# Padding the rows of three large scratch tensors in memory

## The chip, the cores and the metric

The kernel runs on one core of one Trainium2 chip. The metric is the device time of one execution in microseconds (us). All data are 32-bit floats.

## The reference, cut to what matters

The input is 16 images of 16 channels, 256 x 256. Two layers follow each other, each added to its own input:

```python
x = x + _L0_conv_ref(_gn(x), L0_conv_weight)
x = x + _L1_conv_ref(_gn(x), ty, tx, weights_pole1, weights_pole2, weights_residue)
```

`_gn` normalizes groups of two channels. The first layer is a 3 x 3 circular convolution with 16 by 16 channels, written in the reference with Fourier transforms. The second is a Laplace neural operator: a 2D Fourier transform `alpha` of every channel, at every frequency a 16 x 16 complex matrix that mixes the channels, an inverse transform, and a second sum of exponentials built from the poles:

```python
alpha = jnp.fft.fft2(x, axes=(-2, -1))
S = jnp.einsum('ikpq,oikp,xikq->oxik', weights_residue, A, Bm)
output_residue1 = jnp.einsum('biox,oxik->bkox', alpha, S)
x1 = jnp.fft.ifft2(output_residue1, s=(Ny, Nx), axes=(-2, -1)).real
...
return x1 + x2 / Nx / Ny
```

## The kernel before, in words

The work goes through four stages, and what one stage leaves for the next is too large for the on-chip memory. It is kept in three scratch tensors in HBM:

- `vD`, four tensors of 128 x 16 channels x (4 images, 2, 256): the result of the first layer, folded into sums and differences of mirrored rows. The first index is the row pair, and one channel's part for it is 8 KB.
- `aD`, 128 x 32 x 4096: the spectrum. The first index is the frequency along y; of its 32 rows two (real and imaginary part) belong to each channel, and a row of 16 KB holds all 256 frequencies along x of all 16 images.
- `yD`, 128 x 32 x (4, 4, 256): the mixed rows, with the same first two indices, a row again 16 KB.

Stage 1, the convolution, is a loop over `g`, 24 steps for each of the 16 images (`conv`, L283). Small matmuls (L297) fill `ps_conv`; ScalarE evicts them to `pair` and `far` (L316); VectorE and GpSimd fold the mirrored rows (`mirror`, L264 and L267); SyncE stores `vD<-pair` (L326) and loads the images two ahead, `xt<-in_x` (L123). Stage 2, the spectrum, goes over 64 units of one channel and four images: `load_v` (L737) reads `s<-vD` three units ahead, `fold`, `lines` (L768, L776) and `columns` (L811) make the transform, and after four units, so once for each channel, L967 stores the 4 MB tile `spec` to `aD`.

Stage 3 mixes. It is a loop over 32 groups `g` of four frequencies, and in each over four steps `n`. A step makes the next group's weights (`sums`, L1024, `spread`), mixes with the present ones (`mix`, L1112), evicts four PSUM tiles to `yt` (L1225), stores `yt` (`store`, L1126, four DMAs of 128 KB in pieces of 1 KB) and loads a part of the next group's spectrum (`load`, L1094 and L1099, pieces of 2 and 1 KB):

```python
for m in range(4):
    o, src = mix(4 * n + m, sg, yt)
    (nc.vector.tensor_copy if m >= (2 if late else 3) else nc.scalar.copy)(o, src)
...
store(g, n, yt)
if g < 31:
    load(g + 1, n, (2, 3) if n == 1 else range(4))
```

`yt` has two buffers, so the eviction of step `n + 2` needs the stores of step `n` landed. `unmix_first` reads the first frequency's rows back from `yD` at the end of the stage, corrects them and writes them again (L1139, L1149).

Stage 4 is the inverse, over 16 channels `k` and four images at a time. Channel 0's rows of `yD` are read in pieces of 256 bytes (`load_images`, L1275), those of later channels a quarter at a time, 1 MB in pieces of 8 KB (`load_quarter`, L1294). `combine` (L1317, L1321) makes `u` on GpSimd, L1353, L1377 and L1378 transform, VectorE adds v (`vl<-vD`, L1302), and L1391 stores the output.

The order of the instructions is written out by hand in each stage. Nearly all transfers are issued by SyncE, in program order, and each waits until the one eight before it has landed.

Of the kernel before, what the change touches and what calls it, by code (L numbers as in the profile page):

```python
# [9 lines left out]
FP = mybir.dt.float32  # L10
# [6 lines left out]
B = 16  # L17
C = 16
N = 256
P = 128  # L20
# [4 lines left out]
def conv_then_laplace_kernel(ctx: ExitStack, tc: tile.TileContext, a: dict, out: bass.AP):  # L25
# [16 lines left out]
    x = a["x"]  # L42

    cp = ctx.enter_context(tc.tile_pool(name="const", bufs=1))
    dp = ctx.enter_context(tc.tile_pool(name="scratch", bufs=1, space=DRAM))
# [17 lines left out]
    proj = cp.tile([P, 2, B, 16, 2], FP, name="proj", tag="proj")  # L63
    jmat = cp.tile([P, 3, P], FP, name="jmat", tag="jmat")

    vD = [dp.tile([P, C, 4, 2, N], FP, name=f"vD{b}", tag=f"vD{b}") for b in range(B // 4)]
    aD = dp.tile([P, 2 * C, N * B], FP, name="aD", tag="aD")
    yD = dp.tile([P, 2 * C, 4, 4, 16 * B], FP, name="yD", tag="yD")
    cD = dp.tile([P, 4, 8, N], FP, name="cD", tag="cD")
    hD = dp.tile([7, 2, 16, C * C * 4], FP, name="hD", tag="hD")  # L70
    eD = [dp.tile([n, P, C, 2, P], FP, name=f"eD{n}", tag=f"eD{n}") for n in (2, 1)]
# [606 lines left out]
    for g in range(24 * B + 3):  # L678
# [3 lines left out]
        b, n = divmod(g, 24)  # L682
        if b + 2 < B and n % 12 in (4, 5, 10, 11):
            h, k = n // 12, (4, 5, 10, 11).index(n % 12)
# [47 lines left out]
    m, n = cols[:, 16:17], cols[:, 17:18]  # L732

    def load_v(i, b0, eng=nc.sync):
        s = sp.tile([P, 4, 2, N], FP, name="s", tag="s")
        for j in range(0, 4, 2):
            eng.dma_start(out=s[:, j : j + 2], in_=vD[b0 // 4][:, i, j : j + 2])  # L737
        return s.rearrange("p b h x -> p h b x")

    def fold(i, b0, s):  # L740


        vf = f1.tile([P, 2, 2, 4, P], FP, name="vf", tag="vf")
        lo, hi = s[:, :, :, 0:P], s[:, :, :, N - 1 : P - 1 : -1]
        for j in range(4):
            nc.vector.scalar_tensor_tensor(
                vf[:, 0, 0, j], lo[:, 0, j], vmr[:, 1, b0 + j, i : i + 1], hi[:, 0, j], ALU.add, ALU.add
            )
        nc.vector.tensor_tensor(vf[:, 0, 1], lo[:, 1], hi[:, 1], ALU.add)


        vq = fp.tile([P, 2, 2, 4, 2, 64], FP, name="vq", tag="vq")

        def again(xo, eng):
            lo, hi = vf[:, xo, :, :, 0:64], vf[:, xo, :, :, P - 1 : 63 : -1]
            eng.tensor_tensor(vq[:, xo, :, :, 0], lo, hi, ALU.add)  # L756
            eng.tensor_tensor(vq[:, xo, :, :, 1], lo, hi, ALU.subtract)  # L757

        again(0, nc.vector)
        nc.vector.tensor_tensor(vf[:, 1], lo, hi, ALU.subtract)  # L760
        again(1, nc.gpsimd)
        return vq.rearrange("p e o b h x -> p e o b (h x)")

    def lines(i, b0, vf, t, j):

        for xo in range(2):
            ps = pa.tile([P, 512], FP, name="ps_y", tag="ps_y")
            nc.tensor.matmul(  # L768
                ps[:, 0:N],
                lhsT=vf[:, xo, 0, j],  # L770
                rhs=tabE[:, 0 : i + 2 : i + 1],
                start=True,
                stop=False,
                skip_group_check=True,
            )
            nc.tensor.matmul(  # L776
                ps[:, P : P + N],
                lhsT=vf[:, xo, 1, j],
                rhs=tabO[:, i : C + 1 : C - i],
                start=False,  # L780
                stop=True,
                skip_group_check=True,
            )
            nc.scalar.activation(  # L784
                t[:, xo, j].rearrange("p l n -> p (l n)"),
                ps[:, 0:384],
                AF.Copy,
                scale=vmr[:, 0, b0 + j, i : i + 1],
            )
# [44 lines left out]
    def first_slots(b0, spec, pairs, qs):  # L834

        flat = spec.rearrange("p r f b -> p (r f) b")
        for (j, even, odd), q in zip(pairs, qs):
            bs = slice(b0 + j, b0 + j + 2)
            nc.vector.tensor_copy(flat[:, 0:385:384, bs], even[:, :, 0])
            nc.gpsimd.tensor_tensor(  # L840
                flat[:, 256:127:-128, bs],
                q[:, :, 0],
                sgn.unsqueeze(2).to_broadcast([P, 2, 2]),
                ALU.mult,
            )

    def project(i, psd):
        for part in range(2):
            cf = coef[part][:, i].rearrange("p k q s -> p (k q s)")
            cf = cf.unsqueeze(1).to_broadcast([P, B, 32])  # L850
            ac = proj[:, part].rearrange("p b m s -> p b (m s)")
            if i == 0:
                nc.vector.tensor_tensor(ac, psd, cf, ALU.mult)
            else:
                pr = prp.tile([P, B, 32], FP, name="pr", tag="pr")
                nc.vector.tensor_tensor(pr, psd, cf, ALU.mult)
                nc.gpsimd.tensor_tensor(ac, ac, pr, ALU.add)
# [20 lines left out]
    def first_constants():  # L878
        omega(omg, omg, rd[:, 1:2])
        nc.vector.tensor_scalar(pims, p2k[:, :, 1], sset, None, ALU.mult)  # L880
        nc.vector.tensor_tensor(prU[:, 0], p2k[:, :, 0], p2k[:, :, 0], ALU.mult)

        nc.vector.tensor_scalar(prU[:, 1], p2k[:, :, 0], m0, -1.0, ALU.mult, ALU.mult)
        nc.vector.tensor_scalar(prU[:, 2], p2k[:, :, 0], m1, -1.0, ALU.mult, ALU.mult)
# [50 lines left out]
    for u in range(len(units) + 1):  # L935
        at = units[u] if u < len(units) else None
        if at is not None:
            now = vq
            t = lp.tile([P, 2, 4, 3, P], FP, name="t", tag="t")
            if u + 1 < len(units):  # L940
                vq = fold(*units[u + 1], loaded.pop(u + 1))
                if u + 3 < len(units):
                    loaded[u + 3] = load_v(*units[u + 3])
                if u < 2:
                    next(rest)
            for j in range(2):
                lines(*at, now, t, j)
        if last is not None:
            i, b0 = last[:2]
            if b0 == 0:  # L950
                spec = (a0, a1)[i % 2].tile([P, 2, N, B], FP, name="spec", tag="spec")
                psd = pd.tile([P, B, 32], FP, name="psd", tag="psd")
            done = columns(*last, spec, psd)
        if at is not None:
            for j in range(2, 4):
                lines(*at, now, t, j)
                if u < 2:
                    next(rest, None)
        if u == len(units) - 4:
            first_constants()  # L960
        if len(units) - 4 < u < len(units):
            next(first_weights)
        if last is not None:
            first_slots(b0, spec, *done)
            if b0 == B - 4:
                project(i, psd)
                (nc.sync if i + 1 < C else nc.scalar).dma_start(  # L967
                    out=aD[:, 2 * i : 2 * i + 2].rearrange("p r n -> p (r n)"),
                    in_=spec.rearrange("p r f b -> p (r f b)"),
                )  # L970
        last = (*at, t) if at is not None else None
    p1.close()
# [443 lines left out]
    for n, (k, b0) in enumerate(units):  # L1416
# [13 lines left out]
        r = rp.tile([P, 4, 2, N], FP, name="r", tag="r")  # L1430
# [169 lines left out]
```

## Time and profile before

| | us |
|---|---|
| median of 3 runs | 2666.38 (2654.53 to 2671.68) |
| the profiled execution | 2667.82 |
| its span, first to last instruction | 2665.7 |
| TensorE busy | 2487.3 (93%) |
| VectorE busy | 1986.5 (75%) |
| ScalarE busy | 1447.7 (54%) |
| GpSimd busy | 1324.7 (50%) |
| SyncE's DMA queue, share of 16 engines | 71.7% |

The profile is of one execution. "PE" is TensorE, "PEld" its weight loads, "DVE" VectorE, "ACT" ScalarE, "POOL" GpSimd and "SPq" the queue of SyncE. "L1112" is a line of the kernel. A line with an arrow, as in `PE ps_mix L1112 <- DMA yD<-yt`, names an instruction that waited and what released it; "issue" stands for waiting that no event of the profile explains. The DMA share is the mean busy share of the core's 16 DMA engines.

### The profile page before, as it was taken

The page shows a single profiled execution, that of the slowest core. Times are in us where ns is not written, and L with a number is a line of the kernel's source. Part 1 is how long each engine was busy: PE and PEld are TensorE (multiplying, and loading weights), DVE is VectorE, ACT ScalarE, POOL GpSimd, SP SyncE. Part 2 cuts the span into 40 slices and gives each one's busy share as a digit, 9 for nine tenths or more (in the row PEclk, how much of TensorE's full clock was granted, in tenths as well). Part 3 has the DMA queues.
Part 4 walks back from the last instruction along what each step waited for, and adds up shares of the span by engine and source line. Part 5 has one row for each costly group of instructions (what it writes and reads, how often), then busy time and mean ns, then how long its engine had stood idle before and what let it go on. Part 6 is the DMA issues. An engine that isn't in the chain of part 4 may idle for free.

```text
span 2665.7 us, 83901 instructions
## 1 busy us (share of the span) xinstructions
PE 2487.3 (93%) x35314; PEld 1883.0 (71%) x35314; DVE 1986.5 (75%) x3805; ACT 1447.7 (54%) x2727; POOL 1324.7 (50%) x1179
## 2 busy tenths in 40 slices
PE   5988999898999999998999999999699999999998
PEld 2544444466777777775777878888588888888887
DVE  7767778847888888888787878888367666666666
ACT  2555566575666666665666666666244444444443
POOL 1333358432333333334476655776546565665653
PEclk9999999998999999999999999999899999999999
DMA  8888778955565556555777777777878888888884
GB/s 271 266 271 269 263 243 284 286 181 188 214 239 224 200 222 237 217 195 217 222 225 217 232 232 216 231 225 234 245 276 288 285 287 292 280 294 275 301 282 171
DMA packets 311351, 653.11 MB, mean 245 GB/s; under 512 B 44566, under 2 KB 159382, under 8 KB 301120
## 3 DMA queue, kind: packets, MB, share of 16 engines
q1 hardware_dynamic: 309936, 640.55, 71.7%
q8 instruction: 278, 4.55, 0.7%
q0 software_dynamic: 896, 3.02, 0.4%
q10 hardware_dynamic: 144, 4.19, 0.4%
q14 instruction: 97, 0.79, 0.1%
HBM read 368.15 MB, written 280.36 MB: 243 GB/s over the span
## 4 chain that ended last, share of the span: by engine, by line
PE 63%; DMA 4%; SPq 3%; DVE 3%; ACT 1%; issue 1%; POOL 1%; DVEq 0%; ACTq 0%; POOLq 0%
PE ps_mix L1112 11%; PE ps_y L768 9%; PE ps_p L1353 9%; PE ps_y L776 8%; PE ps_f L1377 8%; PE ps_f L1378 8%; PE ps_x L811 4%; DMA yD<-yt 3%; PE ps_s L1024 3%; PE ps_h L1337 2%; SPq L1126 2%; PE psd L796 1%; SPq L1094 1%; DVE sg L1044 1%; ACT yt L1225 0%
## 5 line engine op out<-in xcount | busy, mean ns | idle before, releaser
L1112 PE MATMUL ps_mix<-abd,sg 128*64 128x128 f32 x8192 | 481.1, 276 | 36.6 <-DMA yD<-yt 19.2
L1112 PEld LDWEIGHTS ps_mix<-abd,sg 128*64 128x64 f32 x8192 | 451.1, 138 | 90.2 <-ACT yt L1225 56.8
L297 PE MATMUL ps_conv<-xt,wc 32*32 32x512 f32 x12288 | 453.0, 618 | 57.6 <-issue 49.6
L1317 POOL TENSOR_TENSOR u<-yk 128x512 f32<-128x512 f32 (+1 forms) x268 | 350.1, 1338 | 291.1 <-PE ps_p L1353 223.9
L297 PEld LDWEIGHTS ps_conv<-xt,wc 32*32 32x32 f32 x12288 | 255.1, 105 | 243.3 <-issue 160.7
L784 ACT ACTIVATE t<-ps_y,vmr 128x384 f32<-128x384 f32 x512 | 297.0, 580 | 163.7 <-PE ps_y L776 163.6
L1044 DVE STREAM_SHUFFLE sg<-ps_s 128x512 f32<-128x512 f32 (+1 forms) x264 | 328.9, 1316 | 0.0
L768 PE MATMUL ps_y<-tabE,vq 128*128 128x256 f32 x1024 | 313.5, 388 | 13.6 <-DVE vq L757 12.1
L267 POOL TENSOR_TENSOR pair<-pair,far 128x1024 f32<-128x1024 f32 x64 | 151.6, 2369 | 345.8 <-DVE pair L264 285.6
L776 PE MATMUL ps_y<-tabO,vq 128*128 128x256 f32 x1024 | 306.0, 380 | 0.0
L1377 PE MATMUL ps_f<-pt,inv 128*128 128x256 f32 x1008 | 301.3, 381 | 0.0
L1378 PE MATMUL ps_f<-hs,ey 128*128 128x256 f32 x1008 | 300.5, 380 | 0.0
L1353 PEld LDWEIGHTS ps_p<-inv,u 128*128 128x128 f32 x2048 | 266.3, 193 | 47.2 <-issue 25.5
L1381 DVE TENSOR_TENSOR r<-ps_f,q 128x256 f32<-128x256 f32 x256 | 107.0, 418 | 254.0 <-ACT q L1380 254.0
L1353 PE MATMUL ps_p<-inv,u 128*128 128x128 f32 x2048 | 279.6, 280 | 10.0 <-POOL u L1321 9.9
L1041 ACT ACTIVATE sg<-ps_s,mcol 128x512 f32<-128x512 f32 (+1 forms) x264 | 179.8, 691 | 193.5 <-DVE sg L1044 123.9
L768 PEld LDWEIGHTS ps_y<-tabE,vq 128*128 128x128 f32 x1024 | 189.7, 191 | 90.1 <-ACT q L824 50.3
L1380 ACT COPY q<-ps_f 128x256 f32<-128x256 f32 x256 | 95.4, 372 | 288.8 <-PE ps_f L1378 284.7
L756 POOL TENSOR_TENSOR vq<-vf 128x512 f32<-128x512 f32 x64 | 81.4, 1271 | 295.0 <-DVE vf L760 272.4
L1355 ACT COPY pt<-ps_p 128x512 f32<-128x512 f32 x256 | 150.0, 586 | 134.2 <-PE ps_p L1353 129.9
L776 PEld LDWEIGHTS ps_y<-tabO,vq 128*128 128x128 f32 x1024 | 195.6, 191 | 27.0
L1225 ACT COPY yt<-ps_mix 128x512 f32<-128x512 f32 x352 | 184.8, 591 | 51.2 <-DMA yD<-yt 35.2
(239 smaller groups left out, 4056.3 us busy)
## 6 DMA issues: line engine op xcount, KB each, us to landing
vD<-pair SPq DMA_DIRECT2D x128, 512.0 KB
yD<-yt SPq DMA_DIRECT2D x512, 128.0 KB
vl<-vD SPq DMA_DIRECT2D x128, 512.0 KB
out_y<-ol SPq DMA_DIRECT2D x128, 512.0 KB
s<-vD SPq DMA_DIRECT2D x126, 512.0 KB
aD<-spec SPq DMA_DIRECT2D x15, 4096.0 KB
yk<-yD SPq DMA_DIRECT2D x60, 1024.0 KB
xt<-in_x SPq DMA_DIRECT2D x96, 516.0 KB
```

Source lines behind the costliest of these rows:

```text
L297: nc.tensor.matmul(acc[r][32 * c : 32 * c + 32], lhsT=ready[b][0][rows, phase, tap], rhs=halves[b][u // 2][rows, q : q + 5 : 4, 2 - tap : ...
L768: nc.tensor.matmul(ps[:, 0:N], lhsT=vf[:, xo, 0, j], rhs=tabE[:, 0 : i + 2 : i + 1], start=True, stop=False, skip_group_check=True,)
L776: nc.tensor.matmul(ps[:, P : P + N], lhsT=vf[:, xo, 1, j], rhs=tabO[:, i : C + 1 : C - i], start=False, stop=True, skip_group_check=True,)
L784: nc.scalar.activation(t[:, xo, j].rearrange("p l n -> p (l n)"), ps[:, 0:384], AF.Copy, scale=vmr[:, 0, b0 + j, i : i + 1],)
L1041: nc.scalar.activation(to[..., k : k + 2], src[odd], AF.Copy, scale=nsgn)
L1044: nc.vector.stream_shuffle(to[..., C + k : C + k + 2], src[1 - odd], swap)
L1112: nc.tensor.matmul(ps[64 * t : 64 * t + 64, j], lhsT=sg[:, f : f + 2].rearrange("p f m -> p (f m)"), rhs=abd[jq][:, :, 2 * t + cc, 2 * jj ...
L1225: (nc.vector.tensor_copy if m >= (2 if late else 3) else nc.scalar.copy)(o, src)
L1317: nc.gpsimd.tensor_tensor(u[:, :, j].rearrange("p b (c n) -> p c b n", c=8), in0, in1, o)
L1353: nc.tensor.matmul(ps[:, at], lhsT=u[:, n], rhs=tab, start=True, stop=True)
L1377: nc.tensor.matmul(ps[:, e], lhsT=tab, rhs=pt[:, e], start=True, stop=False)
L1378: nc.tensor.matmul(ps[:, e], lhsT=ey[:, e], rhs=hs, start=False, stop=True)
```

## The change

Behind each row of `aD` and `yD` now lie 256 unused numbers (1 KB), and behind each frequency's 32 rows another 1024 (4 KB). Behind each channel's 8 KB of `vD` lie 256 unused numbers. The distance from row to row grows from 16 to 17 KB in `aD` and `yD`, from frequency to frequency from 512 to 548 KB, in `vD` from channel to channel from 8 to 9 KB and from row pair to row pair from 128 to 144 KB. The store of the spectrum names its two rows one by one, since they no longer touch. All else is as it was.

```diff
-    vD = [dp.tile([P, C, 4, 2, N], FP, name=f"vD{b}", tag=f"vD{b}") for b in range(B // 4)]
-    aD = dp.tile([P, 2 * C, N * B], FP, name="aD", tag="aD")
-    yD = dp.tile([P, 2 * C, 4, 4, 16 * B], FP, name="yD", tag="yD")
+    def pitched(name, rows, row, *split):
+
+        t = dp.tile([P, rows * (row + 256) + 1024], FP, name=name, tag=name)
+        t = t[:, 0 : rows * (row + 256)].rearrange("p (r n) -> p r n", r=rows)[:, :, 0:row]
+        return t.rearrange("p r (i j n) -> p r i j n", i=split[0], j=split[1]) if split else t
+
+    vD = []
+    for b in range(B // 4):
+        t = dp.tile([P, C, 8 * N + 256], FP, name=f"vD{b}", tag=f"vD{b}")
+        vD.append(t[:, :, 0 : 8 * N].rearrange("p c (b h x) -> p c b h x", b=4, h=2))
+    aD = pitched("aD", 2 * C, N * B)
+    yD = pitched("yD", 2 * C, N * B, 4, 4)
...
                 (nc.sync if i + 1 < C else nc.scalar).dma_start(
-                    out=aD[:, 2 * i : 2 * i + 2].rearrange("p r n -> p (r n)"),
-                    in_=spec.rearrange("p r f b -> p (r f b)"),
+                    out=aD[:, 2 * i : 2 * i + 2], in_=spec.rearrange("p r f b -> p r (f b)")
                 )
```

## The prediction

> **What bounds the kernel now.** I read the page first, then the busy time by stage, then the waits of TensorE alone, then the waits inside the mixing stage, and last the trace's records of single DMA packets. The page gives the shares:
>
> ```profile
> span 2665.7 us, 83901 instructions
> PE 2487.3 (93%) x35314; PEld 1883.0 (71%) x35314; DVE 1986.5 (75%) x3805; ACT 1447.7 (54%) x2727; POOL 1324.7 (50%) x1179
> ...
> q1 hardware_dynamic: 309936, 640.55, 71.7%
> ```
>
> TensorE is busy for 93% of the span and SyncE's DMA queue for 72%. So a faster memory can only give back what TensorE idles: 2665.7 - 2487.3 = 178 us in all. Where these lie is told by the windows (columns: stretch, its length, busy us and instructions of PE, PEld, DVE, ACT, POOL, then granted clock, DMA share, GB/s):
>
> ```profile
> 60.00:600.00 540.00, 481.56 (x12041) 265.51 (x12040) 375.34 (x756) 321.35 (x580) 240.78 (x184) 0.97 0.79 259
> 600.00:625.00 25.00, 14.41 (x52) 11.27 (x52) 16.25 (x38) 8.39 (x15) 6.94 (x5) 0.66 0.76 267
> 625.00:1230.00 605.00, 604.66 (x4113) 434.15 (x4112) 511.42 (x1173) 367.32 (x634) 220.24 (x279) 1.00 0.56 214
> ...
> 1260.00:1850.00 590.00, 562.02 (x11438) 475.94 (x11435) 482.49 (x863) 384.57 (x642) 369.12 (x281) 0.99 0.77 226
> 1850.00:1940.00 90.00, 65.80 (x820) 56.81 (x816) 35.58 (x49) 31.42 (x63) 44.97 (x58) 0.85 0.83 247
> 1940.00:2620.00 680.00, 677.96 (x5644) 582.12 (x5643) 464.40 (x647) 295.59 (x705) 414.28 (x351) 1.00 0.83 284
> ```
>
> The spectrum stage (625 to 1230 us) leaves TensorE 0.3 us idle and the inverse stage (1940 to 2620 us) 2.0 us. Nothing that a DMA gains there can reach the end, although DMA is busiest in the inverse stage (0.83). What is left: the convolution, 540 - 481.6 = 58 us; the mixing, 590 - 562 = 28 us; the turn to the inverse, 90 - 65.8 = 24 us; start, end and the two other turns, about 66 us, which are chains of statistics, table work and single round trips. Who ends TensorE's waits (columns: total us, times, longest):
>
> ```profile
> PE ps_conv L297 <- issue: 49.6, 27, 3.7
> PE ps_mix L1112 <- DMA yD<-yt: 19.2, 20, 2.4
> ...
> PE ps_mix L1112 <- ACT yt L1225: 12.8, 8, 7.7
> ```
>
> In the convolution 49.6 of 58 us end in "issue", a wait that no semaphore explains. The packet records show what lies beside: before most of these pauses a 16 KB packet of the instruction queue lands (1.0 to 1.5 us each), for example at 147.3 us, with TensorE going on at 148.8 us after a pause of 3.7 us. TensorE is waiting for its own instructions, which come through the same busy DMA engines. In the mixing the wait is for stores of the mixed rows: `yt` has two buffers, and the eviction two steps later needs the first one's four stores landed. The same wait is seen one engine earlier:
>
> ```profile
> ACT yt L1225 <- DMA yD<-yt: 22.1, 24, 3.4
> ...
> DVE yt L1225 <- DMA yD<-yt: 11.3, 8, 2.9
> ```
>
> So the mixing runs at the edge: from issue to the last semaphore increment of a `yD` store the trace has 3.44 us in the median and 2.44 us for the fastest tenth, against a step of 3.64 us of mixing matmuls and 1.02 us of sums.
>
> **How slow are the packets now?** This decides how much a new layout can give. By the packet records, a 4096-byte packet takes 159 ns in the median, up to the 90th percentile, in the spectrum and in the inverse stage: 4096 / 159 ns x 16 engines = 412 GB/s. The 1 KB packets of the mixing take 46 ns in the median and 55 in the mean, the 2 KB ones 84 and 108, the 2 KB packets of the convolution 84 and 99, the 8 KB reads of `yD` in the inverse 328 and 428 (309 at best). The bulk of every kind goes at its full rate; only a tail of 10 to 25% is late.
>
> **What the Trainium skill says.** "DMA: Bandwidth & Descriptors", section "Latency and other measured facts", has a row on HBM row pitch at large powers of two: copies with a pitch of 512 KiB per partition ran at 207 GB/s, at 2 MiB 164, at 4 MiB 103, and 4 KiB of padding brought 214 back. The pitches here are 512 KB (`aD`, `yD`) and 128 KB (`vD`), so by that row 3% is at stake in a transfer at most, and the trace agrees: the medians are at full rate. It does not cover 1 KB pieces scattered at 16 KB and 512 KB, as in the `yD` stores. The same page, section "How a descriptor splits into AXI transactions", lets a piece cost more only when it does not start on a 256-byte boundary; all padded rows start at multiples of 1 KB, so no piece gets an extra transaction. No run here shows that part yet.
>
> **The change part by part.**
>
> The instructions. On every engine order, shapes and waits are as before, except that each of the 16 stores of the spectrum (L967) names 2 rows of 4096 numbers where it named one of 8192, so 16 KB pieces where 32 KB ones were. A 32 KB piece took 1222 ns in the median; two halves at the same rate take the same. Issuing one took 320 ns, a two-row store like `vD<-pair` 416: 0.1 us x 16 = 1.5 us, on SyncE, in a stage where SyncE is busy for 74 of 605 us. Cost: nothing.
>
> The addresses. `vD`: 8 to 9 KB per channel, 128 to 144 KB per row pair. `aD` and `yD`: 16 to 17 KB per row, 512 to 548 KB per frequency. Bytes moved stay at 640 MB. Only the late tail can change, and by stage it is worth:
>
> 1. Mixing. 1 KB packets hold 0.534 of the engines' time, 2 KB ones 0.21. With every packet at its median that becomes 0.534 x 46/55 + 0.21 x 84/108 = 0.447 + 0.163, so 0.13 less of the stretch, or 0.6 us in a step of 4.7 us. I take half, 0.3 us, since the tail also comes from loads and stores mixing, which stays. The 20 waits of TensorE for `yD` stores (1 us each) and a few of those behind ACT become 0.3 us shorter: 24 x 0.3 = 7 us. The clock falls to half for 3.4 us after two of the longest (at 1416 and 1597 us); without them it costs 2 x 1.7 less; I count 3. Sum: -10 us. Bounds: 0, and -28 us if all idle time goes.
> 2. Convolution. The 2 KB stores of `vD` hold 0.392 of the engines' time, 14% of it late, so the load falls from 0.79 by 0.055 at most, 7%. If the instruction blocks come sooner by the same part, 49.6 x 0.07 = 3.5 us, and 1 us of the nine clock dips there (9 x 1.7 = 15 us). ACT and POOL waits for `vD<-pair` (41 us on POOL) lie beside TensorE's work. -4.5 us. Bounds: 0, and -40 us.
> 3. Turn to the inverse. The 256-byte reads of `yD` run at 18 ns median, 20 mean, and the rest is a round trip of four small loads and stores; -1 us.
> 4. Spectrum and inverse: 0. TensorE hides them; this cover is gone only when the DMA share reaches 1, so for the inverse when packets get longer by 1/0.83, 20%.
>
> Sum: -15.5 us. The profiled execution took 2667.8 us (span 2665.7 and 2.1 around it), so 2652.3 us; it lies 1.4 us above the median of 2666.4, on whose scale this is 2651.
>
> **The rivals.**
>
> A, the forecast: a slightly shorter tail, 2651 us, 2640 to 2662; chance 0.28.
>
> B, nothing happens: the addresses were spread well enough already, and the tail is reads and writes meeting. For it speak the medians at full rate, against it that the strided 1 and 2 KB stores have a tail where the plain 4 KB ones have none at the 90th percentile. 2666 us; chance 0.15.
>
> C, the tail was the layout's: store and load pieces at 16 KB and 512 KB fall on few memory channels, and the padding frees them. Then the mixing loses most of its idle time (-22 and 3 of clock), and with shorter queues the instruction blocks come in time for half the pauses of the convolution (-25 and -8 of clock). 2666 - 58 = 2608 us. For it: the skill's row, and that the `yD` reads at 512 KB are late in the largest part. Against: those same 8 KB reads take 313 ns, full rate, when issued early at 1920 us with less beside them. Chance 0.34.
>
> D, slower. One mechanism: pieces that lay within one aligned 4 KB now cross such a border and rows that began alike now meet on the same channel, so packets get longer, first of all in the mixing. There DMA is busy for 0.77 and each DMA waits for the one eight before it. It decides when the mean 1 KB packet passes 55 x 1/0.77 = 71 ns: then the DMA sets the step. At 80 ns a step is 4.7 x 80/71 = 5.3 us, 0.55 us more, x 128 steps = +70 us, and the pauses of the convolution grow too. Some 2735 us; at a smaller excess 2700. Nothing in the profile speaks for it but the thin margin; the full rate of today can only be kept or lost, which is why I give it 0.23.
>
> That the change does not do what it says is excluded by the instruction lists: the transfers name the new strides, and no wait appears.
>
> **How the numbers follow.** About 1%, 27 us, is what a measurement of this kernel can tell from no change. A and B lie within it (0.43). C is faster by over 1% (0.34), D slower (0.23). Of the small-effect cases A is the likelier, and with B beside it the centre of the chance: 2651 us, own range 2640 to 2662. The range for 8 in 10 leaves out a tenth on each side: down to 2603 for the larger part of C, up to 2712 for the nearer part of D.
>
> **What would show it right or wrong.** The mean 1 KB packet in the mixing should fall from 55 to about 50 ns, the 2 KB one from 108 to about 95, and the wait of `ps_mix` for `yD<-yt` from 19.2 us to about 12. The windows of spectrum and inverse should keep their lengths within 2 us. It is wrong if the means stay and the time moves all the same, if "issue" in the convolution falls by more than 15 us (then C), or if the DMA share rises in any stage with TensorE's idle time (then D).

## The result, and the profile after

The changed kernel takes 2657.62 us in the median (2645.82 to 2667.38), the kernel before 2667.9 us. The ratio is 0.9961, with a 95% interval of 0.9948 to 0.9974: 10 us faster, 0.4%. The forecast was 2651 us, 15.5 us below before, within 1%.

The page of the profile after:

```profile
span 2643.7 us, 83901 instructions
PE 2483.2 (94%) x35314; PEld 1880.4 (71%) x35314; DVE 1983.8 (75%) x3805; ACT 1450.5 (55%) x2727; POOL 1327.4 (50%) x1179
...
q1 hardware_dynamic: 311856, 640.55, 71.7%
```

The profiled execution (2645.8 us) lies 12 us under the median of its kernel, that of before 2 us under its own. So the two profiles differ by 22 us where the kernels differ by 10, and no single stage's difference of a few us may be taken at its word: there is one profile of each kernel. The number of packets rose by 1920, which is 15 times 128: the 32 KB pieces of SyncE's 15 spectrum stores became two each.

The windows of after, same columns as before:

```profile
60.00:600.00 540.00, 480.77 (x11993) 264.81 (x11975) 385.62 (x766) 323.80 (x582) 245.07 (x184) 0.96 0.76 265
600.00:625.00 25.00, 23.29 (x131) 16.95 (x129) 19.39 (x54) 12.67 (x23) 7.89 (x8) 0.89 0.44 154
...
1260.00:1850.00 590.00, 564.78 (x11504) 478.15 (x11501) 481.22 (x863) 388.94 (x647) 377.57 (x287) 0.99 0.78 227
1850.00:1940.00 90.00, 70.47 (x714) 60.99 (x711) 34.23 (x52) 29.75 (x67) 47.01 (x58) 0.89 0.93 268
1940.00:2620.00 680.00, 678.96 (x5661) 584.67 (x5660) 463.47 (x648) 296.36 (x705) 409.68 (x353) 1.00 0.82 283
```

A fixed window misleads once a kernel is earlier: the convolution of after ends inside the first row, so its busy time looks unchanged there. The row from 600 to 625 us shows it: TensorE is busy for 23.3 us where before it was for 14.4, because the spectrum has already begun. Better is where the first spectrum matmul starts. The lines of the tile `ps_y` give it (min/median/max ns, then first and last start), before and then after:

```profile
L768 PE MATMUL ps_y<-tabE,vq x1024: 379/379/797, 609.0 to 1224.2; 128*128 128x256 f32 x171
```

```profile
L777 PE MATMUL ps_y<-tabE,vq x1024: 379/379/793, 599.0 to 1214.0; 128*128 128x256 f32 x171
```

Ten us are won before the spectrum starts. The spectrum itself takes 615 us in both. TensorE's waits after:

```profile
PE ps_conv L306 <- issue: 37.2, 26, 5.0
PE ps_mix L1120 <- DMA yD<-yt: 17.7, 15, 2.7
...
PE ps_mix L1120 <- ACT yt L1233: 9.5, 6, 7.5
```

The convolution's "issue" waits fell from 49.6 to 37.2 us; the mixing's wait for the `yD` stores hardly, from 19.2 to 17.7. The packet records: 2 KB packets of the convolution 93.5 ns in the mean (99.0 before), the image loads of 2064 bytes 94.2 (99.4), the 1 KB packets of the mixing 55.9 (55.0). By the semaphore increments, the stores of v land 5.2 us after their issue in the median (6.4 before), the `yD` stores 3.2 (3.4), the loads of `aD` 3.9 and 2.9 (4.5 and 3.2). "Landing" is the time from a transfer's issue to its last semaphore increment; a packet's time is that of one piece.

My theory after seeing this: each stage gains from its own tensor, the convolution from `vD`, the mixing from `aD` and `yD`. The rivals: only one of the tensors counts; or no layout counts, and a shift of where the tensors begin does.

### The profile page after: what moved, and what is told of

Read it like the earlier page. It is cut to its first block, busy times and chain, and to the rows that moved or that the text cites. A ratio compares the mean times of both kernels' runs of the same rounds, so it can differ in the third digit from the quotient of the medians.

```text
span 2643.7 us, 83901 instructions
## 1 busy us (share of the span) xinstructions
PE 2483.2 (94%) x35314; PEld 1880.4 (71%) x35314; DVE 1983.8 (75%) x3805; ACT 1450.5 (55%) x2727; POOL 1327.4 (50%) x1179
## 4 chain that ended last, share of the span: by engine, by line
PE 61%; DMA 5%; DVE 4%; SPq 4%; ACT 2%; issue 1%; POOL 1%; ACTq 0%; DVEq 0%; POOLq 0%
PE ps_mix L1120 9%; PE ps_y L777 9%; PE ps_p L1361 9%; PE ps_y L785 8%; PE ps_f L1385 8%; PE ps_f L1386 8%; PE ps_x L820 5%; DMA yD<-yt 4%; PE ps_s L1032 2%; SPq L1134 2%; PE ps_h L1345 2%; PE psd L805 1%; DVE sg L1052 1%; ACT yt L1233 1%; SPq L1102 1%
## 5 line engine op out<-in xcount | busy, mean ns | idle before, releaser
L1120 PE MATMUL ps_mix<-abd,sg 128*64 128x128 f32 x8192 | 480.7, 276 | 32.5 <-DMA yD<-yt 17.7
L306 PE MATMUL ps_conv<-xt,wc 32*32 32x512 f32 x12288 | 453.5, 618 | 45.2 <-issue 37.2
```

The source lines that it names most:

```text
L306: nc.tensor.matmul(acc[r][32 * c : 32 * c + 32], lhsT=ready[b][0][rows, phase, tap], rhs=halves[b][u // 2][rows, q : q + 5 : 4, 2 - tap : ...
L1120: nc.tensor.matmul(ps[64 * t : 64 * t + 64, j], lhsT=sg[:, f : f + 2].rearrange("p f m -> p (f m)"), rhs=abd[jq][:, :, 2 * t + cc, 2 * jj ...
```

## The experiments

### Which tensor: vD alone, aD and yD alone

```diff
# vD alone: the changed vD, and
-    aD = pitched("aD", 2 * C, N * B)
-    yD = pitched("yD", 2 * C, N * B, 4, 4)
+    aD = dp.tile([P, 2 * C, N * B], FP, name="aD", tag="aD")
+    yD = dp.tile([P, 2 * C, 4, 4, 16 * B], FP, name="yD", tag="yD")
...
# aD and yD alone: the changed aD and yD, and vD as before
```

> Only vD is padded; aD and yD lie as before. Theory 1 (each stage gains from the tensor it stores and loads): the convolution keeps its gain (stage from the first conv matmul to the first of the spectrum about 570 us where before has 580), the mixing stage stays at before's 651 us, total about 6 us below before. Theory 2 (the gain is one of aD and yD, the convolution's shorter time in the profile is chance): total equal to before within 2 us, landing of vD<-pair stays at 6.4 us in the median.

> aD and yD are padded, vD is as before. Theory 1: convolution as before (580 us, issue waits of TensorE about 50 us), landing of the yD stores 3.2 us in the median as in the changed kernel (3.44 before), mixing about 647 us, total about 4 us below before. Theory 2: total as the changed kernel, about 10 us below before. Rival (no layout effect in either, the difference is a shift of base addresses): landing 3.4 us and the time anywhere between the two.

`vD` alone: 2650.38 us, ratio 0.9927 (0.9898 to 0.9955). `aD` and `yD` alone: 2677.75 us, ratio 1.0023 (1.0007 to 1.0038). The theory falls for the mixing: the padding of `aD` and `yD` does not bring its share, it costs. With `vD` alone, TensorE's waits in the convolution are those of the whole change:

```profile
PE ps_conv L300 <- issue: 38.4, 28, 4.4
```

and with `aD` and `yD` alone those of before:

```profile
PE ps_conv L303 <- issue: 53.3, 31, 4.8
```

The mixing's landings moved as expected all the same, `yD` stores 3.1 us and loads of `aD` 4.0 and 3.0 us, but TensorE's wait for `yD<-yt` stayed at 17.2 us. A shorter landing of 0.3 us was worth nothing there.

### Which distance: without the 4 KB, and larger powers of two

```diff
# without the 4 KB
-        t = dp.tile([P, rows * (row + 256) + 1024], FP, name=name, tag=name)
+        t = dp.tile([P, rows * (row + 256)], FP, name=name, tag=name)
# larger powers of two
+        t = dp.tile([P, rows * (4 * row)], FP, name=name, tag=name)
...
+        t = dp.tile([P, C, 4 * 8 * N], FP, name=f"vD{b}", tag=f"vD{b}")
```

> All three padded by 1 KB a row, but the 4 KB behind each frequency of aD and yD left out (544 KB instead of 548 KB per frequency). If the scattering of the rows is what counts: same as the changed kernel within 2 us, yD stores land in 3.2 us. If the four frequencies of one store must be kept apart by the odd 4 KB: mixing back at 651 us and landing back at 3.4 us, total about 4 us above the changed kernel.

> The opposite layout: gaps that make the distances larger powers of two (64 KB per row and 2 MB per frequency in aD and yD, 32 KB per channel and 512 KB per row pair in vD). If power-of-two distances load few memory channels: all landings longer than before, yD stores 4.5 us or more, the mixing above 680 us, the total over 2750 us. If the distances do not matter and only mixing of reads and writes makes the tail: within 1% of before, landings within 0.2 us.

Without the 4 KB: 2656.99 us, ratio 0.9945 (0.9921 to 0.9970), not to be told from the change; the `yD` stores land in 3.2 us. The 4 KB does nothing that these runs can tell.

The larger powers of two: 2671.67 us, ratio 1.0009 (0.9989 to 1.0028), and it hides two things that cancel:

```profile
PE ps_conv L306 <- issue: 40.9, 33, 4.8
PE ps_mix L1120 <- DMA yD<-yt: 23.9, 18, 3.4
```

The convolution is as short as with padding (first spectrum matmul at 598.4 us), though 32 KB per channel is a power of two like 8 KB. The rest is longer: TensorE's wait for `yD<-yt` is 23.9 us, and in the inverse the transfers are no longer hidden behind TensorE's work. Busy time of TensorE from 1950 to 2600 us, before and then wide:

```profile
1950.00:2600.00 650.00, 648.74 (x5393) 557.90 (x5392) 442.20 (x619) 283.09 (x674) 395.01 (x336) 1.00 0.84 287
```

```profile
1950.00:2600.00 650.00, 640.59 (x5323) 549.71 (x5315) 438.19 (x612) 279.90 (x666) 390.32 (x336) 0.99 0.84 286
```

TensorE idles 9.4 us there instead of 1.3. Both of my expectations missed: it was not over 2750 us, and not a case of no effect. A power of two as such is not what made the convolution slow.

### Beginnings or distance: vD shifted, vD at 16 KB

```diff
# shifted: 8 KB per channel as before, 1033 KB behind each of the four tensors
+        t = dp.tile([P * C * 8 * N + 256 * 1033], FP, name=f"vD{b}", tag=f"vD{b}")
+        t = t[0 : P * C * 8 * N].rearrange("(p c b h x) -> p c b h x", p=P, c=C, b=4, h=2)
# 16 KB per channel
-        t = dp.tile([P, C, 8 * N + 256], FP, name=f"vD{b}", tag=f"vD{b}")
+        t = dp.tile([P, C, 8 * N + 8 * N], FP, name=f"vD{b}", tag=f"vD{b}")
```

> Layouts inside all tensors as before (8 KB per channel of vD), but 1033 KB of unused memory behind each of the four vD tensors, so that their beginnings, and those of aD and yD, lie elsewhere. Theory P (the 8 KB distance between channels is what costs): as before, 2669 us, convolution 580 us or more. Theory S (it was the distance of 16 MB between the tensors or the beginnings): as with vD padded, about 2650 us, convolution 568 us.

> vD alone with 16 KB per channel instead of 9 KB (256 KB per row pair), aD and yD as before. If any distance other than 8 KB helps, since the pieces of one store then no longer fill one closed megabyte: as with 9 KB, about 2650 us and a convolution of 568 us. If powers of two hurt: as before, 2669 us. The wide layout, also a power of two, had a convolution of 569 us, so the first is expected.

Shifted: 2672.88 us, ratio 1.0015 (1.0001 to 1.0028); no gain. At 16 KB, with `aD` and `yD` as before: 2654.53 us, ratio 0.9948 (0.9932 to 0.9963); the gain. First the shifted, then the 16 KB kernel:

```profile
PE ps_conv L301 <- issue: 54.2, 30, 5.1
```

```profile
PE ps_conv L300 <- issue: 40.5, 33, 4.2
```

So it is the distance between the pieces of a store, and 8 KB is the bad one; 9, 16 and 32 KB are alike. (In every layout the row pairs lie 16 times as far apart as the channels, so these two distances were not separated.) Where the tensors begin is not it, as far as one shift can tell.

### The price of aD and yD: one at a time, and the change without aD

```diff
# yD alone: vD and aD as before.  aD alone: vD and yD as before.
# vD and yD: the change without
-    aD = pitched("aD", 2 * C, N * B)
+    aD = dp.tile([P, 2 * C, N * B], FP, name="aD", tag="aD")
```

> Only yD is padded. With aD and yD padded the kernel was 0.23% slower than before, 6 us. Theory T (the price is the 256-byte reads of yD at the turn, 24 instead of 18 ns, 12544 of them over 16 engines, 4.3 us): about 2674 us here too, with the packets at 24 ns. Theory A (the price is the spectrum's, stored in two 16 KB pieces): as before, 2669 us.

> Only the spectrum aD is padded, and stored as two rows of 16 KB. With aD and yD padded the kernel was 0.23% slower, with yD alone equal to before. If the price is aD's: 0.2% slower, 2675 us. If it was chance (both intervals come close to 0.1%): within 0.1% of before.

> The change without its part on aD: vD and yD padded. If aD's padding costs 6 us: about 2650 us, as with vD alone, 0.7% below before. If nothing but vD counts and the rest is chance: between 0.4 and 0.7% below before, with no order among the versions that pad vD.

`yD` alone: 2668.55 us, ratio 0.9994 (0.9979 to 1.0009). Its 256-byte packets do take 24 ns instead of 18, but that costs nothing that these runs can tell: this theory of the price falls. `aD` alone: 2682.23 us, ratio 1.0054 (1.0039 to 1.0069), 14 us slower, more than expected. `vD` and `yD`: 2649.02 us, ratio 0.9927 (0.9907 to 0.9946), as fast as `vD` alone, with the convolution's waits again below those of before:

```profile
PE ps_conv L306 <- issue: 42.9, 30, 4.2
```

So the price is `aD`'s, and the change without it is faster than before and, by intervals that just fail to overlap, faster than the change. How large the price is depends on what else is padded: 14 us alone, 6 us with `yD`, about 9 us between the change and the change without `aD`; the change without the 4 KB lies between those two. The landings name `aD` as well: with `yD` alone padded its stores land in 3.44 us, as before, with `aD` alone in 3.26 us. What the padding of `aD` shortened was not what the kernel waited for.

Where `aD`'s padding costs is open. In its profile the longest part lies ahead of the first use of `aD`, in the convolution:

```profile
PE ps_conv L303 <- issue: 61.6, 34, 4.8
```

against 52 to 54 us for `yD` alone, for the shifted kernel and for `aD` and `yD` together, which has `aD` padded too. The spectrum and mixing stages of the two profiles with `aD` padded and `vD` as before are longer by 1 to 3 us each, but the spectrum is not in the two where `vD` is padded too. What `aD`'s size moves in memory, behind it, are the tables' scratch tensors `cD`, `hD` and `eD`, of which the convolution uses two; but `yD` and the shifted `vD` move them as well. One profile for each is too little to say more.

### The transfers by themselves

```diff
# no computing; in each part, for each layout, one kind of transfer after the other
+    for turn in range(2):
+        for part in (store_y_alone, load_y_alone, both_y, store_v_alone, load_v_alone, ...):
+            for y, v in sets:
+                part(y, v)
...
# second kernel: 64 image loads and 64 stores of v in turn, then 32 stores alone, for each layout
+        for part in (together, stores):
+            for v in sets:
+                part(v)
```

> No computing: only the transfers of the scratch tensors, each kind alone, twice, on three layouts (plain as before; padded as in the change; wide as in the larger powers of two). It leaves out the whole calculation and writes zeros, so only the landings and packets count. Theory V (the layout of vD costs its stores even when nothing runs beside them): stores of v in the plain layout land later than in the padded and the wide one by at least 5%. Theory N (layout matters only among other traffic): equal within 2%. For the mixed rows: stores and loads of 1 KB together land 0.2 to 0.3 us later in the plain layout if the shorter landing of the changed kernel is the layout's; 256-byte reads take 24 to 25 ns in the padded layout and 18 in the plain and wide ones if that price is the layout's.

> No computing: the convolution's transfers alone, image loads and stores of v in turn and then the stores by themselves, for four distances between v's channels (8, 9, 16 and 32 KB), twice. It leaves out the whole calculation and writes zeros. In the whole kernel the three wider distances made the convolution 19 us shorter, yet by themselves the stores at 8 KB landed sooner (5.9 us against 7.1). Theory R (stores at 8 KB get in the way of the loads beside them): loads and stores together take at least 4% longer at 8 KB than at the others. Theory I (what they get in the way of is the instruction blocks or the small traffic of the tables, not the loads): together, 8 KB is as fast as the others or faster.

In the first kernel the sign is reversed: stores of v alone land in 6.1 us in the plain layout and 7.2 in the padded one. The issues' table (tile, queue, count, size, median us to landing):

```profile
yplain<-yt SPq DMA_DIRECT2D x512, 128.0 KB, 2.5
ypadded<-yt SPq DMA_DIRECT2D x512, 128.0 KB, 2.4
...
abd<-yplain SPq DMA_DIRECT2D x512, 128.0 KB, 2.9
abd<-ypadded SPq DMA_DIRECT2D x512, 128.0 KB, 2.7
...
vplain<-pair SPq DMA_DIRECT2D x64, 512.0 KB, 6.1
vpadded<-pair SPq DMA_DIRECT2D x64, 512.0 KB, 7.2
vwide<-pair SPq DMA_DIRECT2D x64, 512.0 KB, 8.6
```

The mixed rows' loads land 0.2 us earlier when padded, and the stores beside loads 0.15 us: that part of the expectation holds, though both gains come at the larger power of two as well. The 256-byte packets took 20 to 21 ns in the median when padded and 18 otherwise, less than the 24 to 25 expected, and eight loads made of them were nevertheless through in 25 us instead of 36. The 1 KB packets take 54 to 58 ns in the mean here too, in every layout, with nothing computing: that tail is no matter of layout.

In the second kernel, image loads and stores of v together, the windows of the four layouts, 8, 9, 16 and 32 KB (here DVE and POOL busy, clock, DMA share, GB/s):

```profile
92.00:269.00 177.00, 0.00 (x0) 0.00 (x0) 1.00 1.05 405
269.00:446.00 177.00, 0.00 (x0) 0.00 (x0) 1.00 1.05 406
446.00:623.00 177.00, 0.00 (x0) 0.00 (x0) 1.00 1.05 406
623.00:799.00 176.00, 0.00 (x0) 0.00 (x0) 1.00 1.05 406
```

All four run at 405 to 406 GB/s; from start to start it is 177.5 us at 8 KB and 176.7 at 9 KB. The stores by themselves took 52 us for 32 at 8 KB and 53 to 54 us at the others. Theory R (the stores hinder the image loads) falls as it was put. And the packets have no tail here: 84.0 ns in the mean for the stores, 85.0 to 85.6 for the loads, against 99 for both in the kernel before. So the distance of 8 KB matters to something that these two streams don't contain, or only when they come as in the kernel: here the DMA engines are never idle, while in the convolution of before their share is 0.79. The second was not tested.

### Half the stores of v

```diff
+            if b % 2 == 0:
                 nc.sync.dma_start(
                     out=vD[b // 4][y : y + 16, :, b % 4].rearrange("(t y) c h x -> (y c) t (h x)", t=2),
```

> The layout of before, but the stores of v are left out for every second image, and the later loads of v read the neighbour image twice; the computing is all there, its values are not the reference's. Theory C (TensorE's issue waits in the convolution, 50 us, come from its instruction blocks arriving late behind the data): with half the stores the issue waits fall below 25 us and the convolution below 565 us, shorter than with padding. Rival (the issue waits belong to the instruction stream itself, whatever the data): they stay at 50 us and the convolution at 580 to 590 us.

2651.46 us, ratio 0.9937 (0.9915 to 0.9958). From 60 to 560 us the DMA share fell to 0.65:

```profile
60.00:560.00 500.00, 450.58 (x11197) 250.32 (x11201) 373.06 (x745) 297.18 (x538) 228.19 (x176) 0.96 0.65 210
```

```profile
PE ps_conv L297 <- issue: 45.6, 25, 4.1
```

The issue waits fell, but to 45.6 us and not below 25, and the convolution took 569 us, no less than with padding. Theory C holds in its direction only. The packets left keep their mean of 99 ns. So a new distance, with every byte stored, does as much for this stage as leaving out half of the stores does at 8 KB.

## Why the prediction was right or wrong

The total was right in sign and size, though the forecast gain was half as large again as the measured one: -15.5 for -10 us. Its terms were not right, so that the total came near is luck: the mixing gave nothing that can be told, the convolution gave more than its term, and `aD` took some back, for which the forecast had no term. By the prediction's own sign of being wrong, "the means stay and the time moves all the same", the mixing's account fails: the mean 1 KB packet stayed at 55.9 ns (about 50 forecast), the 2 KB one went from 108 to 106 (95), the wait for `yD<-yt` to 17.7 us (12).

The stages of the profiles, from the first matmul of one stage to the first of the next, in us:

| | convolution | spectrum | mixing and turn | inverse |
|---|---|---|---|---|
| before | 579.6 | 644.6 | 651.0 | 761.1 |
| the change | 569.7 | 644.4 | 646.8 | 753.5 |
| vD alone | 568.2 | 646.5 | 644.7 | 759.3 |
| vD and yD | 570.1 | 644.3 | 648.2 | 758.8 |
| vD at 16 KB | 567.7 | 644.4 | 649.1 | 761.5 |
| vD shifted | 589.9 | 644.5 | 652.0 | 753.4 |
| yD alone | 589.6 | 644.6 | 646.7 | 759.9 |
| aD and yD | 592.4 | 647.3 | 653.5 | 758.8 |
| aD alone | 592.4 | 646.9 | 652.0 | 759.7 |
| all, larger powers of two | 569.0 | 644.4 | 656.8 | 769.1 |
| the change without the 4 KB | 568.8 | 644.6 | 653.9 | 760.2 |
| half the stores | 569.1 | 644.5 | 650.4 | 763.2 |

**Step 1, mixing, -10 us: failed.** The term was built on 1 KB packets coming down from 55 to their median; they went to 55.9, and the transfers by themselves show that tail in every layout. What the padding did shorten is the landing, by 0.25 us for stores, close to the 0.3 us that I had put in, and that came with `aD`'s layout and not with `yD`'s own. But neither the wait for `yD<-yt` nor the stage followed: the wait is 17.2 us with `aD` and `yD` padded and 17.6 with `vD` alone, the stage 653.5 us and 644.7 us.

**Step 2, convolution, -4.5 us: mis-sized.** Of the kernels that make every store, the five with 8 KB per channel lie at 579.6 to 592.4 us, the six others at 567.7 to 570.1. The means are 588.8 and 568.9: -20 us. The profile of before was the shortest of its kind, and the six lie 9.5 to 12 us below it; the timed gain of `vD` alone is 19 us at 9 KB and 15 at 16 KB. So the term was too small by a factor of two to four. I had priced the pauses by the share of DMA load that the tail makes, 7% of 49.6 us. By the records, between the first matmul of the stage and the first of the spectrum TensorE is idle for 78 us in the mean of the five and for 63 us in the six, of which "issue" makes 56 and 41, and busy for 511 and 506 us. So 15 of the 20 us are waits for instructions, and the other 5 go with the halved clock, whose stretches of 3.4 us begin mostly (81 of 101 in all profiles) within 2 us of the end of a pause above 0.8 us. In the profile of before an instruction block lands within 18 of the 22 "issue" pauses above 0.8 us, and TensorE resumes 1.46 us after the last block in the median (1.4 to 1.5 us in every other profile). The Trainium skill, "Runtime: NRT & Kernel Launch", section "Terms", says that each engine's instruction memory is refilled in blocks of 16 KiB; the trace has 98 such packets of 16384 bytes from 40 us to the end of the convolution. So the place and the mechanism on TensorE's side were right, and the size of the layout's hold on it was not. The working had also counted nine stretches at half clock in this stage, where the records have ten.

**Step 3, turn, -1 us:** not to be told; the 256-byte packets got slower, 18 to 24 ns, where I had expected nothing, and `yD` alone shows no cost that these runs can tell.

**Step 4, spectrum and inverse, 0:** held for the spectrum, 644.4 and 644.6 us; the inverse left the 2 us that the prediction allowed, with 753.5 us for 761.1, but the shifted kernel has 753.4 with every distance as before, so this need not be the layout's. It is clearly longer only at the larger powers of two, 769 us.

**Rivals.** C, the large gain, had the convolution's waits for instructions in it, at -33 us too large, and the mixing wrong; that few memory channels are the reason was not shown, and a larger power of two, 32 KB, did not slow the convolution. B's statement, that the addresses are spread well enough, holds for the mixed rows. D's place was wrong: the mean 1 KB packet of the mixing stayed below 57 ns in every kernel, where D needed 71 (and its step grows by 0.6 us, which makes 76 us and not 70). But a slower side exists, in `aD`.

**The pitch of the rows.** By the row on pitch in the Trainium skill, "DMA: Bandwidth & Descriptors", section "Latency and other measured facts", 3% of a transfer was at stake at 512 KB and nothing was said of 8 KB between pieces; read alone it points to `aD` and `yD`, and the runs put the gain in `vD`. Its lower rate at 2 MiB is seen: eight loads of 1 MB in 8 KB pieces, with nothing computing, took 20 us from start to start at 548 KB and 24 to 25 us at 2 MB.

**What stays open.** Why a distance of 8 KB between 2 KB pieces delays TensorE's instructions. With an always full queue the image loads and the stores are equally fast in all layouts and free of a tail; in the kernels they are not: stores of v land after 6.3 to 6.7 us in the five 8 KB kernels and after 4.9 to 5.3 us in the six others, the image loads after 8.0 to 8.5 and 7.3 to 7.5 us. The instruction blocks themselves take some 1090 to 1110 ns in the first and 1050 to 1080 ns in the second. But 30 ns on 98 blocks is 3 us, not 20, and half the stores leave 1110 ns with a short convolution. What differs more is when a block begins. Count the instructions that TensorE has started and take off 256 for each block that has begun (278 blocks serve its 71000 instructions): in all profiles this count stops at 449, where TensorE has run dry. In the five, 12 to 17 of the 98 blocks begin within ten of that limit, in the six 6 to 10, with half the stores 9. So this points to blocks that begin late, more than to blocks that take long. What holds it back, and whether it meets a store in memory, was not shown. Open too is where `aD`'s 14 us arise.

## What to carry to other kernels

Before padding, ask which wait would become shorter: here transfers of all three scratch tensors landed earlier, and only one wait, of an engine for its own instructions, gave time back. Undo a layout change one tensor at a time: a gain of 15 to 19 us and a loss of 6 to 14 us came together as 10. And test the transfer alone only beside the whole kernel: stores of v alone were slower in the layout that made the kernel faster.

## What the runs showed of the hardware that was not expected

- TensorE's "issue" pauses in a stage of small matmuls depend on where another engine's stores go: 49.6 to 61.6 us with 2 KB pieces 8 KB apart, 37.2 to 42.9 us at 9, 16 or 32 KB, all bytes stored.
- Of transfers alone, the closest layout is not the slowest: 512 KB stores landed in 6.1 us at 8 KB, 7.2 at 9 KB and 8.6 at 32 KB. Beside image loads, with the queue always full, all landed in 10.9 us.
- 256-byte pieces took 24 ns in the median instead of 18 in the kernels whose `yD` has 17 KB rows 544 or 548 KB apart, while those of 1, 2 and 4 KB kept their median (46, 84 and 159 ns).
